# Weight folding around a branch: four pairs ahead of it instead of two, four buffers, and unread matrix products

## The chip, the cores and the metric

The kernel runs on one core of a Trainium2 chip. The metric is the device time of one execution in microseconds (us). Three runs of the kernel before took 677.29, 679.67 and 687.41 us; the median is 679.67 us. All times inside the kernel come from one profiled execution of the same kernel and are counted from the start of its span.

## The reference, cut to what matters

Two layers work on 800 tokens (8 batches of 100) of width 512, with a context of 361 rows of width 128:

```
x = x + L0_xattn(layernorm(x), ctx)      # 16 heads, causal mask over the first 100 context rows
x = x + L0_ffn(layernorm(x))             # 8 experts, each token to its best 2
x = x + L1_xattn(layernorm(x), ctx)      # low-rank queries, see below
x = x + L1_ffn(layernorm(x))             # weights and activations rounded to 8-bit steps
```

The part that matters here is the query path of the third line:

```
q_hk  = (hidden_q @ Wq.T).reshape(b, s, H, K)          # 16 heads of 128
q_big = einsum('bshk,hkq->bshq', q_hk, w_kc_q)         # to 384
q_r   = einsum('bshq,hqr->bhsr', q_big, W_qr)          # to 64 per head
```

None of the three matrices depends on the input, so the kernel multiplies them into one matrix `wqf` (512 x 1024) first, two heads ("a pair") at a time: eight pairs in all. This is called folding. Folding needs nothing but weights, so it can be put wherever TensorE would wait. The mixture of experts is the second line:

```
scores = einsum('btd,ed->bte', x, Wg)
topk_s, topk_i = top_k(scores, 2)
probs = softmax(topk_s)
y += w[..., e] * (silu(x @ W1[e].T) * (x @ W2[e].T)) @ W3[e].T     # for each expert e
```

## The kernel before, in words

TensorE (PE), VectorE (DVE) and ScalarE (ACT) run in the order in which the source writes their instructions (`tc.manual_schedule`); SyncE's queue (SP) issues nearly all transfers, and GpSimd (POOL) the indirect ones. A tile scheduler orders SP's transfers; in the built program each SP transfer waits for the one eight before it, as eight semaphores go round.

**Folding a pair.** `fold_load` (L698) issues five transfers for a pair on SP: `wq_p` (512 KB), and for each of two heads `kq_p` (192 KB) and `qr_p` (96 KB): 1088 KB. `fold_first` (L722) makes six products 128x64 (`kq_p` by `qr_p`, L711, twelve matmul instructions in the trace) and copies the result to `a_p` with ACT (L719). `fold_second` (L746) multiplies `a_p` by `wq_p` (L749, four instructions) and copies it to `f_p` with ACT (L753). `fold_third` (L756) turns `f_p` with four transposes (L759) and copies into `wqf` with ACT (L760). Inside the experts, `fold_beside` (L727, L731) and `fold_turn` (L739, L741) replace `fold_first`. The pool `fold_in` (L493) has three buffers for a pair's weights.

**Ahead of the branch.** After the first attention the kernel ranks the experts for each token. Tiles 0 to 4 of 128 tokens go first, tiles 5 and 6 later: `gate_norm` (L557) writes a normalised tile on DVE and issues a transfer `x_acc<-x` on SP; `gate_columns` (L569) transposes (L578), `gate_scores` (L586) makes the scores (L593, L601), `rank_choices` (L611) picks two experts with a chain of small DVE operations, `give_slots` (L653) counts with two products (L658, L661) where a token goes, and issues one indirect write on POOL per tile and choice (L686, 13 in all) into `x_slot` in HBM. Weights of experts 0 and 1 and of fold pairs 0, 1, 2 are loaded before that. Between the steps the kernel folds pair 0 and, later, pair 1. Pair 3 is loaded once pair 0 has been folded.

**The branch** (L906 to L1004). If an expert got more than 240 tokens, a loop handles what did not fit. With these inputs it is not entered; every engine reads one number (`spilt`, L831) and jumps past it.

**Behind the branch.** SP fetches the rows of experts 0 and 1 from `x_slot` (`fetch`, L1012; L1015), which needs the last indirect write to have landed; behind them three `gu` tiles and one `dn` tile of the last layer's weights, and pair 4 (`while len(loaded) < 3`, L1082). PE folds pairs 2 and 3 meanwhile, and then transposes the rows of expert 0 (`columns_of`, L1035; L1040).

**The experts** (L1102). For each: gate and up products in three parts (L1109), down products (L1175), scaling, and an indirect add into `x_acc` on POOL (L1186). Expert 0 to 3 each fold one pair between these steps (pairs 4 to 7, `fold_beside` behind the first of the three parts), and each issues the load of a later pair. DVE also rounds the last layer's weights there: two `gu` tiles per expert (`quantise_next`) and, in experts 0 to 3, one `dn` tile (`quantise_down`, L147 first) between the second and the third part's multiplication (L1133). There is one buffer for `dn`, so tile n+1 is loaded once tile n is rounded and turned. Weights of expert e+2 are loaded when expert e has finished with the buffer (`load_expert`, L482), and from expert 5 on the loads `wo` (L1070) use fold buffers that have come free.

Of the kernel before, what the change touches and what calls it, by code (L numbers as in the profile page):

```python
# [12 lines left out]
F32 = mybir.dt.float32  # L13
# [6 lines left out]
P = 128  # L20
# [30 lines left out]
def tile_kernel(  # L51
# [438 lines left out]

    fw, close_fw = open_pool("fold_in", bufs=3, side="right")  # L493
    wqf = fold.tile([P, KC, NH1 * R1], F32, tag="wqf", name="wqf")

    gp, close_gp = open_pool("gate", side="right")
# [225 lines left out]
    def fold_first(*loads):  # L722
        pa = fold_head(*loads, 0)
        return fold_copy(*loads, fold_head(*loads, 1, pa))
# [34 lines left out]
            nc.tensor.transpose(pt[:, ts(c, P)], f_p[:, ts(c, P)], ident)  # L759
        nc.scalar.copy(wqf[:, :, ts(i, P)], pt.rearrange("p (c r) -> p c r", c=KC))  # L760

    pairs_left = list(range(3, NH1 // 2))
    loaded = [fold_load(i) for i in range(3)]


    begin(6)
# [36 lines left out]
    project_part(5, po, oT, wout_sb, KC, 0, KC)  # L803
    rank_choices(0, 5)
    give_slots(0, 5)
    part = fold_first(*loaded.pop(0))
    project_add(5, po)
    token_stats(mvs, 5, 6)
    token_scales(mvs, sd_all, rstd_all, 5, 7)
    nc.scalar.activation(sd0[:, 0:1], ln_eps, AF.Exp)  # L810
    for t in range(5, 7):
        gate_norm(t)
    part = fold_second(*part)
    loaded.append(fold_load(pairs_left.pop(0)))
    xT = gate_columns(5, 7)
    fold_third(*part)
    gate_scores(5, 7, xT)

    part = fold_first(*loaded.pop(0))
    rank_choices(5, 7)  # L820
    give_slots(5, 7)

# [6 lines left out]
    nc.vector.tensor_reduce(most, pn[:, :NE], AX.X, ALU.max)  # L829
    spilt = gp.tile([P, 1], I32, tag="spilt", name="spilt")  # L830
    nc.vector.tensor_scalar(spilt, most, float(CAP), None, ALU.is_gt)  # L831
    part = fold_second(*part)
    fold_third(*part)
    close_atw()
    close_at()

# [76 lines left out]
    with tc.If(spills > 0, preferred_fallthrough_block=True):  # L913


        sp, close_sp = open_pool("spill", side="right")
        wts = sp.tile([P, NT, NE], F32, tag="wts", name="wts")
        for k in range(2):
            nc.vector.scalar_tensor_tensor(
                probs[k], slot1[k], 0.0, probs[k], ALU.is_equal, ALU.mult  # L920
            )
            nc.vector.tensor_tensor(
                hots[k], hots[k], probs[k].unsqueeze(2).to_broadcast([P, NT, NE]), ALU.mult
            )
        nc.vector.tensor_tensor(wts, hots[0], hots[1], ALU.add)
        full = N // P
        nc.gpsimd.memset(xs[0], 0.0)
        nc.gpsimd.dma_start(
            x_all_rows[: full * P].rearrange("(t p) d -> p t d", p=P), x_all[:, :full, :D]
        )  # L930
        nc.gpsimd.dma_start(x_all_rows[full * P : N], x_all[: N - full * P, full, :D])
        nc.gpsimd.dma_start(x_all_rows[N:], xs[0][: NR - N])
        for e in range(NE):
            nc.gpsimd.dma_start(
                spilt_gates[ds(e * NR, NR)].rearrange("(t p) o -> p t o", p=P),
                wts[:, :, e].unsqueeze(2),
            )

        at_w = sp.tile([P, KC + 3], I32, tag="at_w", name="at_w")
        nc.gpsimd.iota(at_w[:, :KC], pattern=[[P, KC]], base=0, channel_multiplier=1)  # L940
        nc.gpsimd.iota(at_w[:, KC:], pattern=[[P, 3]], base=0, channel_multiplier=1)
        at_x = sp.tile([P, 1], I32, tag="at_x", name="at_x")
        at_g = sp.tile([P, 1], I32, tag="at_g", name="at_g")
        nc.gpsimd.iota(at_g, pattern=[[0, 1]], base=0, channel_multiplier=1)

        def gathered(dst, src, at):
            nc.gpsimd.indirect_dma_start(
                out=dst, out_offset=None, in_=src,
                in_offset=bass.IndirectOffsetOnAxis(ap=at, axis=0),
            )  # L950

        with tc.For_i(0, NE, 1, hint_engines=()):
            nc.gpsimd.iota(at_x, pattern=[[0, 1]], base=0, channel_multiplier=1)
            w12_e = sp.tile([P, KC, 2 * HE], F32, tag="spw", name="spw")
            for c in range(KC):
                gathered(w12_e[:, c, :], w12.rearrange("e d h -> (e d) h"), at_w[:, c : c + 1])
            w3_e = sp.tile([P, 3, D], F32, tag="sp3", name="sp3")
            for m, (m0, mr) in enumerate(HCH):
                gathered(
                    w3_e[:mr, m, :], w3.rearrange("e h d -> (e h) d"),  # L960
                    at_w[:mr, KC + m : KC + m + 1],
                )
            nc.vector.tensor_scalar(at_w[:, :KC], at_w[:, :KC], D, None, ALU.add)
            nc.vector.tensor_scalar(at_w[:, KC:], at_w[:, KC:], HE, None, ALU.add)
            with tc.For_i(0, NT, 1, hint_engines=()):
                x_t = sp.tile([P, D], F32, tag="spx", name="spx")
                gathered(x_t, x_all_rows, at_x)
                g_t = sp.tile([P, 1], F32, tag="spg", name="spg")
                gathered(g_t, spilt_gates, at_g)
                pt = bank()  # L970
                for c in range(KC):
                    nc.tensor.transpose(pt[:, ts(c, P)], x_t[:, ts(c, P)], ident)
                xT = sp.tile([P, KC, P], F32, tag="spxT", name="spxT")
                nc.scalar.copy(xT, pt.rearrange("p (c q) -> p c q", c=KC))
                hT = sp.tile([P, 3, P], F32, tag="sph", name="sph")
                for m, (m0, mr) in enumerate(HCH):
                    pw = bank()
                    ups = [(0, UP[m], mr)] if m < 2 else [(0, UP64, 64), (64, HE, 32)]
                    for j, cols in enumerate(([(0, m0, mr)], ups)):
                        for to, at_col, n in cols:  # L980
                            for c in range(KC):
                                nc.tensor.matmul(
                                    pw[ds(to, n), ds(j * P, P)], w12_e[:, c, ds(at_col, n)],
                                    xT[:, c, :], start=(c == 0), stop=(c == KC - 1),
                                )
                    s = sp.tile([P, P], F32, tag="sps", name="sps")
                    nc.scalar.activation(s[:mr], pw[:mr, :P], AF.Silu)
                    nc.vector.tensor_tensor(hT[:mr, m, :], s[:mr], pw[:mr, ds(P, P)], ALU.mult)
                py = bank()
                for m, (m0, mr) in enumerate(HCH):  # L990
                    nc.tensor.matmul(
                        py[:, :D], hT[:mr, m, :], w3_e[:mr, m, :], start=(m == 0), stop=(m == 2)
                    )
                y_t = sp.tile([P, D], F32, tag="spy", name="spy")
# [84 lines left out]
    behind_slots.__enter__()  # L1079
    gate_up_in = [load_gate_up(gate_up_left.pop(0)) for _ in range(GB)]  # L1080
    down_in = load_down(0)
    while len(loaded) < 3:  # L1082
        loaded.append(fold_load(pairs_left.pop(0)))


# [4 lines left out]
    in_order.__enter__()  # L1090

    nc.scalar.activation(most, ln_eps, AF.Silu)
    part = fold_first(*loaded.pop(0))
    following = fold_first(*loaded.pop(0))
    part = fold_second(*part)
    following = fold_second(*following)
    fold_third(*part)
    fold_third(*following)
    turned = columns_of(0, slots[0])
    gates = choices(0, slots[0])  # L1100

# [709 lines left out]
```

## Time and profile before

| | us |
|---|---|
| median of three runs | 679.67 |
| profiled execution, device time | 681.28 |
| its span | 679.5 |
| PE busy | 646.9 (95%) |
| DVE busy | 419.9 (62%) |
| ACT busy | 245.0 (36%) |
| POOL busy | 183.5 (27%) |
| mean granted TensorE clock | 0.973 of full |

The profiled execution is 1.61 us above the median, and 1.78 us of it lie outside its span. Busy PE is not PE at its peak: at half clock the same products count twice the busy time. A line of the timeline reads: start, duration, engine, source line, operation, output and inputs, shape, how many instructions the line merges, and in brackets how long the engine was idle before it and what ended that. "SPq" is the issue of a transfer, not the transfer itself. In the table of stretches each row gives, after its length, the busy time and the number of instructions for PE, weight loads, DVE, ACT and POOL, and then the granted clock, the mean busy share of the 16 DMA engines, and GB/s.

### The profile page before, as it was taken

The numbers are of one execution on the slowest core, as the hardware profiler recorded it, in microseconds if no ns is written. First come the engines' busy times: TensorE is split into PE (matmuls) and PEld (weight loads), VectorE is DVE, ScalarE is ACT, GpSimd is POOL, SyncE is SP. The second block draws the span as 40 slices with busy tenths as digits, with TensorE's granted clock in tenths as the row PEclk, the third lists the DMA queues.
The fourth block names the chain that finished last, engine by engine and source line by source line (L and its number), as shares of the span: only waits on it lengthen the run. The fifth ranks groups of instructions, "written<-read, shape, count | busy, mean of one in ns | idle before, by whom it ended". The sixth has DMA issues, their size and how long they took to land.

```text
span 679.5 us, 9904 instructions
## 1 busy us (share of the span) xinstructions
PE 646.9 (95%) x3476; PEld 415.3 (61%) x3483; DVE 419.9 (62%) x1065; ACT 245.0 (36%) x565; POOL 183.5 (27%) x196
## 2 busy tenths in 40 slices
PE   8999997889998999999989999999999999999994
PEld 5766755666655677568866666666666544444442
DVE  4875697326655553353148877876677356666687
ACT  3654544322222111232145555555555313222140
POOL 2222231501110122138514243244234102221020
PEclk9999999589999999999989999999999999999998
DMA  9700393699999998654200211110000210011211
GB/s 292 249 18 17 119 322 108 241 309 220 299 295 302 253 326 214 140 175 120 84 1 15 59 44 21 53 36 12 0 13 0 90 38 20 18 30 29 49 37 63
DMA packets 80290, 80.35 MB, mean 118 GB/s; under 512 B 41267, under 2 KB 54119, under 8 KB 80111
## 3 DMA queue, kind: packets, MB, share of 16 engines
q1 hardware_dynamic: 76543, 70.97, 36.6%
q0 software_dynamic: 3696, 8.72, 6.0%
q8 instruction: 29, 0.48, 0.3%
q14 instruction: 22, 0.18, 0.1%
HBM read 56.36 MB, written 16.50 MB: 107 GB/s over the span
## 4 chain that ended last, share of the span: by engine, by line
PE 63%; DVE 7%; DMA 7%; POOL 1%; issue 1%; ACT 1%; SPq 0%; ACTq 0%; POOLq 0%; DVEq 0%
PE bank L359 12%; PE bank L1406 9%; PE bank L1379 9%; PE bank L1109 8%; PE bank L1325 6%; PE bank L1175 5%; PE bank L1394 5%; PE bank L1539 3%; DMA dn<-in_wdn 2%; PE bank L1361 1%; DMA gu<-in_wgu 1%; DMA qr_p<-in_wqr 1%; POOL e L1388 1%; DVE amax L147 1%; PE bank L711 1%
## 5 line engine op out<-in xcount | busy, mean ns | idle before, releaser
L1388 POOL TENSOR_SCALAR e<-e,rs 128x361 f32<-128x361 f32 (+1 forms) x56 | 67.2, 1201 | 131.9 <-DVE rs L1387 118.7
L359 PE MATMUL bank<-wvo,ctxT 128*128 128x512 f32 x192 | 83.9, 593 | 0.0
L1379 PE MATMUL bank<-kvT,qe 128*128 128x361 f32 (+1 forms) x208 | 83.0, 483 | 0.1
L1109 PE MATMUL bank<-xgT,w 128*128 128x240 f32 (+1 forms) x384 | 76.5, 373 | 1.6 <-ACT xgT L1044 0.9
L1109 PEld LDWEIGHTS bank<-xgT,w 128*128 128x128 f32 (+1 forms) x384 | 64.7, 183 | 14.4 <-issue 5.6
L1406 PE MATMUL bank<-pT,kvr 121*128 121x400 f32 x192 | 70.3, 502 | 1.0 <-DVE pT L80 1.0
L1394 PEld LDWEIGHTS bank<-ident,e 128*121 128x121 f32 (+1 forms) x312 | 48.3, 186 | 34.2 <-POOL e L1388 7.3
L1385 ACT ACTIVATE e<-bank,nm 128x361 f32<-128x361 f32 (+1 forms) x104 | 58.7, 565 | 27.2 <-DVE nm L1381 18.9
L1381 DVE TENSOR_REDUCE nm<-bank 128x1 f32<-128x361 f32 (+1 forms) x104 | 54.9, 528 | 15.8 <-PE bank L1379 14.6
L359 PEld LDWEIGHTS bank<-wvo,ctxT 128*128 128x128 f32 x192 | 36.2, 190 | 43.0 <-issue 42.6
L1186 POOL DMA_INDIRECT x_acc<-y,place x16 | 24.5, 1530 | 129.9 <-ACT y L1185 126.2
L1394 PE MATMUL bank<-ident,e 128*121 128x128 f32 (+1 forms) x312 | 53.0, 280 | 3.1 <-POOL e L1388 3.0
L1556 POOL TENSOR_TENSOR hid<-g,u 128x512 f32<-128x512 f32 (+1 forms) x17 | 20.5, 1216 | 111.0 <-ACT g L1547 74.8
L1175 PE MATMUL bank<-w,hT 128*128 128x512 f32 (+3 forms) x96 | 44.3, 607 | 4.0 <-DVE hT L1133 4.0
L1406 PEld LDWEIGHTS bank<-pT,kvr 121*128 121x128 f32 x192 | 33.9, 190 | 20.2 <-ACT pT L82 0.7
L1325 PE MATMUL bank<-xT,wqf 128*128 128x256 f32 (+1 forms) x192 | 43.8, 389 | 0.7 <-ACT xT L1310 0.7
L82 ACT COPY pT<-bank 121x384 f32<-121x384 f32 (+1 forms) x63 | 28.2, 447 | 42.4 <-PE bank L1394 42.3
L324 POOL TENSOR_TENSOR s<-s,rs 100x800 f32<-100x800 f32 x16 | 24.4, 1522 | 70.0 <-DVE rs L323 30.5
L1325 PEld LDWEIGHTS bank<-xT,wqf 128*128 128x128 f32 x192 | 36.3, 190 | 7.4 <-ACT xT L1310 0.9
L80 DVE COPY ctxT<-bank 128x400 f32<-128x400 f32 (+2 forms) x31 | 17.7, 572 | 37.0 <-PE bank L1325 26.0
L1379 PEld LDWEIGHTS bank<-kvT,qe 128*128 128x128 f32 (+1 forms) x208 | 32.9, 189 | 10.7 <-DVE rs L1387 0.5
L1175 PEld LDWEIGHTS bank<-w,hT 128*128 128x128 f32 (+3 forms) x96 | 16.8, 184 | 25.1 <-issue 16.6
(259 smaller groups left out, 1004.2 us busy)
## 6 DMA issues: line engine op xcount, KB each, us to landing
w<-in_w SPq DMA_DIRECT2D x8, 1408.0 KB
gu<-in_wgu SPq DMA_DIRECT2D x22, 256.0 KB
w<-in_w SPq DMA_DIRECT2D x16, 256.0 KB
wq_p<-in_wq SPq DMA_DIRECT2D x8, 512.0 KB
wo<-in_wo SPq DMA_DIRECT2D x8, 512.0 KB
x_slot<-zeros SPq DMA_DIRECT2D x1, 3840.0 KB
kq_p<-in_wkcq SPq DMA_DIRECT2D x16, 192.0 KB
dn<-in_wdn SPq DMA_DIRECT2D x4, 704.0 KB
```

The costliest lines, as they stand in the source:

```text
L82: nc.scalar.copy(dst, src)
L359: nc.tensor.matmul(po[:, :D], lhs[:, c, ds(t * P, r)], rhs[:, c, :], start=(c == 0), stop=(c == chunks - 1),)
L1109: nc.tensor.matmul(po, w12_e[:, c, cols], xgT[:, c, :], start=(c == c0), stop=(c == c1 - 1))
L1175: nc.tensor.matmul(py[i][:n], hT[:mr, m, ds(s0, n)], w3_e[:mr, m, :], start=(m == 0), stop=(m == 2))
L1186: d = nc.gpsimd.indirect_dma_start(out=x_acc, out_offset=bass.IndirectOffsetOnAxis(ap=place[:, 0:1], axis=0), in_=y, in_offset=None, compu ...
L1325: nc.tensor.matmul(pq[:, i, :], wqf[:, c, ts(p0 + i, P)], xT[:, c, :], start=(c == 0), stop=(c == KC - 1),)
L1379: nc.tensor.matmul(ps[:r, :L], qe[:, ds(k0, r)], kvT, start=True, stop=True)
L1381: d = nc.vector.tensor_reduce(nm[:r], ps[:r, :L], AX.X, ALU.max, negate=True)
L1385: nc.scalar.activation(e[:r], ps[:r, :L], AF.Exp, bias=nm[:r], accum_out=sm[:r])
L1388: (nc.vector if odd else nc.gpsimd).tensor_scalar_mul(e[:r], e[:r], rs[:r])
L1394: nc.tensor.transpose(pt[:LP, c, :r], e[:r, ds(c * (LP - 1), LP)], ident[:r, :r])
L1406: nc.tensor.matmul(pc[:, :VC], kvr[:, c, :], pT[:, c, :], start=(c == 0), stop=(c == LC - 1))
```

## The change

Four pairs are loaded at the start instead of three, into four buffers; pairs 0 to 3 are folded ahead of the branch and only pair 4 behind it; pairs 5, 6 and 7 are all loaded right behind the branch, and folded in experts 0, 1 and 2. Behind the branch four products 128x512 whose results nobody reads stand between the steps of pair 4 and before the rows' transposes. They multiply `ident` with a part of expert 0's weights, which are long loaded. To make room, the loop for tokens that do not fit uses older tiles as buffers; it is not entered here.

```
-    fw, close_fw = open_pool("fold_in", bufs=3, side="right")
+    fw, close_fw = open_pool("fold_in", bufs=4, side="right")
...
-    pairs_left = list(range(3, NH1 // 2))
-    loaded = [fold_load(i) for i in range(3)]
+    pairs_left = list(range(4, NH1 // 2))
+    loaded = [fold_load(i) for i in range(4)]
...
     give_slots(0, 5)
-    part = fold_first(*loaded.pop(0))
+    pair0 = fold_first(*loaded.pop(0))
     project_add(5, po)
...
     for t in range(5, 7):
         gate_norm(t)
-    part = fold_second(*part)
+    pair0 = fold_second(*pair0)
     loaded.append(fold_load(pairs_left.pop(0)))
+    pair1 = fold_first(*loaded.pop(0))
     xT = gate_columns(5, 7)
-    fold_third(*part)
+    pair1 = fold_second(*pair1)
     gate_scores(5, 7, xT)
 
-    part = fold_first(*loaded.pop(0))
+    pair2 = fold_first(*loaded.pop(0))
+    fold_third(*pair0)
+    fold_third(*pair1)
     rank_choices(5, 7)
     give_slots(5, 7)
...
-    part = fold_second(*part)
-    fold_third(*part)
+    pair2 = fold_second(*pair2)
+    pair3 = fold_first(*loaded.pop(0))
+    fold_third(*pair2)
+    pair3 = fold_second(*pair3)
+    fold_third(*pair3)
...
-    while len(loaded) < 3:
+    behind_branch = loaded.pop(0)
+    while pairs_left:
         loaded.append(fold_load(pairs_left.pop(0)))
...
-    part = fold_first(*loaded.pop(0))
-    following = fold_first(*loaded.pop(0))
-    part = fold_second(*part)
-    following = fold_second(*following)
-    fold_third(*part)
-    fold_third(*following)
+
+    def at_work(n):
+        for _ in range(n):
+            nc.tensor.matmul(bank(), ident, experts[0][0][:, 0, :512], start=True, stop=True)
+
+    pair4 = fold_first(*behind_branch)
+    at_work(1)
+    pair4 = fold_second(*pair4)
+    at_work(1)
+    fold_third(*pair4)
+    at_work(2)
+    part = None
     turned = columns_of(0, slots[0])
```

In the built program's order on SP, the five transfers of pair 3 now stand ahead of the writes `x_acc<-x` of tiles 2, 3, 4 and 6, and the fifteen transfers of pairs 5, 6 and 7 stand between the first `dn` tile and the fetch of expert 2's rows. The loads of expert 2's gate and up weights move behind the transpose of the first rounded `dn` tile, and each `wo` load moves up by one expert.

More of the change, by code (lines that the diff above doesn't have):

```diff
@@ L937, in tile_kernel @@
             )
+        w12_at = x_all.rearrange("p t w -> p (t w)")[:, : KC * 2 * HE]
+        w12_at = w12_at.rearrange("p (c h) -> p c h", c=KC)
         at_w = sp.tile([P, KC + 3], I32, tag="at_w", name="at_w")
@@ L953, in tile_kernel @@
             nc.gpsimd.iota(at_x, pattern=[[0, 1]], base=0, channel_multiplier=1)
-            w12_e = sp.tile([P, KC, 2 * HE], F32, tag="spw", name="spw")
+            w12_e = w12_at
             for c in range(KC):
                 gathered(w12_e[:, c, :], w12.rearrange("e d h -> (e d) h"), at_w[:, c : c + 1])
-            w3_e = sp.tile([P, 3, D], F32, tag="sp3", name="sp3")
+            w3_e = xs[1:4]
             for m, (m0, mr) in enumerate(HCH):
                 gathered(
-                    w3_e[:mr, m, :], w3.rearrange("e h d -> (e h) d"),
+                    w3_e[m][:mr], w3.rearrange("e h d -> (e h) d"),
                     at_w[:mr, KC + m : KC + m + 1],
@@ L965, in tile_kernel @@
             with tc.For_i(0, NT, 1, hint_engines=()):
-                x_t = sp.tile([P, D], F32, tag="spx", name="spx")
+                x_t = xs[4]
                 gathered(x_t, x_all_rows, at_x)
@@ L991, in tile_kernel @@
                     nc.tensor.matmul(
-                        py[:, :D], hT[:mr, m, :], w3_e[:mr, m, :], start=(m == 0), stop=(m == 2)
+                        py[:, :D], hT[:mr, m, :], w3_e[m][:mr], start=(m == 0), stop=(m == 2)
                     )
-                y_t = sp.tile([P, D], F32, tag="spy", name="spy")
+                y_t = xs[5]
                 nc.vector.tensor_scalar(y_t, py[:, :D], g_t, None, ALU.mult)
```

## The prediction

> **What bounds the kernel now.** PE is busy 95% of the span, so I looked first for where it is not, or is slow. The page's slices show one clock dip that matters, at 119 to 136 us, the place of the change.
>
> ```profile
> PEclk9999999589999999999989999999999999999998
> ```
>
> (One digit per 17 us.) Then the table of stretches: where the clock changed, and how much PE worked in some stretches of 3.41 us.
>
> ```profile
> 117.60:117.70 0.10, 0.00 (x0) 0.00 (x0) 0.10 (x1) 0.10 (x1) 0.00 (x0) 0.89 1.18 221
> 141.50:141.60 0.10, 0.10 (x2) 0.10 (x1) 0.00 (x0) 0.10 (x1) 0.00 (x0) 0.66 0.76 307
> ...
> 353.10:353.20 0.10, 0.10 (x4) 0.10 (x3) 0.00 (x0) 0.00 (x0) 0.00 (x0) 0.98 0.00 0
> 356.60:356.70 0.10, 0.10 (x3) 0.10 (x2) 0.10 (x1) 0.00 (x0) 0.00 (x0) 0.96 0.00 0
> ...
> 114.28:117.69 3.41, 1.29 (x6) 0.27 (x5) 2.77 (x12) 2.17 (x4) 2.21 (x2) 1.00 0.45 123
> 216.67:220.09 3.42, 0.99 (x3) 0.51 (x4) 3.20 (x9) 0.00 (x0) 0.00 (x0) 1.00 1.10 346
> 131.34:134.76 3.42, 3.42 (x18) 3.42 (x17) 0.00 (x0) 1.06 (x3) 0.26 (x1) 0.50 0.33 81
> 138.17:141.58 3.41, 3.41 (x14) 1.71 (x11) 0.00 (x0) 1.68 (x3) 0.00 (x0) 0.50 1.03 323
> ```
>
> The clock (third from the right) falls at 117.69, rises at about 141.53, falls at 353.20, rises at 356.60. These lie 23.84, 211.67 and 3.40 us apart, near multiples (7, 62, 1) of 3.41: the clock is set on a grid. It fell behind a cell with 1.29 us of PE (L711, L749), yet not behind one with 0.99 us of wide products (L1175); a cell full of L711, 64 columns each, did not lift it, a cell of L749 and transposes did. Wide products count, fold products little.
>
> The timeline then gives the events around the branch:
>
> ```profile
> 118.19 1.68 PE L578 MATMUL bank<-ident,x_all 128*128 128x128 f32 x8 [2.27 <-DVE x_all L560]
> 130.69 0.91 POOL L686 DMA_INDIRECT x_slot<-x_all,to  x1 [0.30 <-DVEq L913]
> 131.02 5.36 PE L711 MATMUL bank<-qr_p,kq_p 128*128 128x64 f32 x24 [1.01 <-PEq L913]
> 134.54 1.76 SPq L1015 DMA_DIRECT2D xg<-x_slot  x4
> 141.63 0.99 PE L1040 MATMUL bank<-ident,xg 128*128 128x128 f32 x8
> 148.62 0.87 PE L731 MATMUL bank<-kq_p,qr_p 128*64 128x128 f32 x10 [0.91 <-DMA qr_p<-in_wqr]
> ```
>
> POOL's thirteen indirect writes run nearly back to back from 115.05 to 131.6, and their landing frees the row fetch at 134.54. PE folds pairs 2 and 3 at half clock until 141.6, does not wait for rows, then waits at L731 for pair 4. The chain of waits shows that this is transfers, and so are two later stalls:
>
> ```profile
> 136.48 4.65 DMA gu<-in_wgu
> ...
> 141.14 7.44 DMA qr_p<-in_wqr
> ...
> 182.76 8.93 DMA dn<-in_wdn
> ...
> 207.03 6.35 DMA dn<-in_wdn
> ```
>
> After those `dn` landings PE waits 0.87 us (expert 2, at 197.42) and 2.88 us (expert 3, at 219.10) for L1133, which DVE does behind `quantise_down`. From 222 to 277 PE runs without a gap.
>
> **Part by part, on the profiled execution's own clock.**
>
> Loading pair 3 early: 1088 KB, 3.3 us at the 330 GB/s of 100 to 104 us. DMA carries only 87 and 18 GB/s at 104 to 112, and the `x_acc` writes it is put ahead of have no reader before the adds at 163. Cost 0. Pair 4 takes pair 3's old place, behind pair 0 (114.5).
>
> Folding ahead of the branch. Full-clock prices from pair 0: L711 1.52, L749 1.08; L759 at half clock 1.11, so about 0.6 (the expert stage has 0.60). Pair 1's L711 runs 115.9 to 117.4, in the 2.27 us gap; its cell then holds 2.8 us of PE instead of 1.29, so I take the clock to stay up. L749 of pair 1, which waits for its copy behind ACT's table load (to 118.7), pushes L593 by about 1 us; full-clock transposes (1.1 for 1.68) and sums win it back. Pair 2's L711 and two thirds (1.2) fit into the DVE chain of 2.7 us from score to L658. The last three indirect writes need their slots by 127.8; they waited 0.33 us, so rows come at most 0.3 earlier. Behind L658: 1.08 + 1.52 + 0.6 + 1.08 + 0.7 (ACT's copy) + 0.6, so PE reaches the branch at about 131.4 rather than 130.0, restarts 1 us later, at 132.4.
>
> Behind the branch: pair 4, 1.52 + 1.08 + 0.6, and four unread products. Their nearest row is L359, where eight instructions (four products) took 3.68 us: 0.92 each, 3.7 in all (6.7 at half clock, by L749's 1.98 to 1.08). That gives 139.0 to 139.3; before, it was 141.63. The rows are there: the transfers of pair 4 wait for the one eight before them, and `kq_p` issued at 138.76, so expert 0's two tiles had landed by about 138.7. So 2.6 us are won here, and the unread products cost at most 0.5.
>
> They are lost at once. Pair 5 now stands where pair 4 stood on SP: rows 968 KB, `gu` 768, `dn` 704, pair 1088, from 135.45 when bytes begin to flow. So L731 starts at 148.3 at best, while PE now arrives at about 144.4. Net gain here 0.3, with an idle 3.9 us instead of 1.2.
>
> That idle can drop the clock. A cell must keep about 1 us of wide work, so an idle of 3.9 escapes in 28% of phases: both ends must hold at least 1.48 of idle, 0.94 of 3.41. One cell at half clock costs up to 1.7 us, two 3.4, none 0: I take 1.6, towards one cell, as at 353.20.
>
> On the page "TensorE: Matmul & The Clock Gate" of the Trainium skill, section "Part 1: The HAM clock gate", the clock halves after a whole idle window of about 3.4 us and returns after one sustained busy window. By it, a gap of 2.27 us could not have halved the clock at 117.7 and 5.36 us of L711 should have restored it; the trace has both otherwise. By the rule an idle of 3.9 rarely holds a whole window, and the sum below would lose its 1.6.
>
> Experts 0 to 3. One pair less: expert 3 drops L731 0.81, L741 0.11, L749 0.86, L759 0.44 = 2.2 us of PE. Transfers: up to expert 2's `dn`, old and new order carry the same 12.9 MB (3.3 of folds plus an early 0.5 `wo` against 3.8 of folds), but pairs 6 and 7 now fill 152 to 158, where DMA moved 97, 260 and 185 GB/s: about 0.7 MB, 2.4 us. From there to expert 3's `dn`, 0.32 MB less (0.58 of pair 7 against 0.26 of `wo` parts), 1.1 us. So both landings come about 3.5 earlier. Bounds: PE gains 0.9 + 2.9 + 2.2 = 6.0 if `dn` keeps up, 0 if it doesn't move. Expert 2's weights are issued some 10 us later (165 for 155.68), and are read from 180: cover about 8 us, cost 0; with that cover gone, each us of delay is one of PE.
>
> Sum at expert 3's end: PE's own chain -0.3 + 1.6 - 6.0 = -4.7, but no earlier than `dn`, -3.5. Experts 4 to 7 and all behind are PE's own and move along. 681.28 - 3.5 = 677.8; the profiled run lies 1.6 above the median, so 676.2.
>
> **Rivals.**
>
> (a) Transfers set the end anyway. For: equal bytes up to expert 2's `dn`, and the `dn` transposes on SP take 4 to 8 us each behind whatever is queued. Against: the lull at 152. The gain shrinks to 0 to 1: about 679.
>
> (b) Everything comes true and neither the clock nor `dn` bites: -0.3 - 6.0 = -6.3, 673.4. Against: the 3.9 us idle.
>
> (c) Slower: the clock falls ahead of the branch all the same, since fold products did not lift it before. Then pair 1's L749 (1.98) and its third (1.11) stand ahead of L658, which comes 3.1 us late; slots, indirect writes and rows follow. Behind L658 come 2.82 + 1.98 + 1.1 + 0.7 more, behind the branch 10 to 13 us for 10.6. L731 comes 8 to 11 late. With all 6.0 regained later: +2; with none: +11. Middle +6, 685.7. It decides from the clock at 118 to 125. Against: the cell is fuller than 1.29, and all cells at 96 to 114 with transposes and narrow products held the clock.
>
> (d) The change doesn't do what it says: rows come later than the products' end, and the clock drops there. It costs 1 to 2, about 681.
>
> **How the numbers follow.** Forecast 0.42, (a) 0.18, (b) 0.12, (c) 0.20, (d) 0.08. I predict 676. The likeliest case alone spans 673 to 680. Range 668 to 687: below, (b) less the 1.6 us that a grid shift could save at 353 and the noise of the runs (2 to 8 us around their median); above, (c). Over 2% (13.6 us, about what these runs can tell from no change) needs (b) plus stretches the profile does not show, 0.08, or the upper end of (c) with a lasting half clock, 0.11. That leaves 0.81 within 2%.
>
> **What would show it.** Clock at full from 112 to 140 with L1040 near 139: the fold ahead of the branch is right; half clock at 118: (c). PE idle near 4 us before L731, ended by `qr_p`, at about 148: the give-back; none there would refute my queue reading. Half clock at about 148 to 152: the 1.6. In experts 2 and 3 no PE wait for L1133 over 1 us: the 3.5; waits as before: (a). Expert 2's first L1109 waiting for weights would break the cover I counted on.

## The result and the profile after

The changed kernel took 678.69 us (median of 20 runs, 675.34 to 686.19), the kernel before 677.31 us in the same runs (20 runs, 675.46 to 687.93). The ratio is 1.0019, with a 95% interval of 0.9996 to 1.0042: no change that can be measured. Measured once more (the third group below), it had 677.16 us against 677.65 for the kernel before, ratio 0.999 [0.9966, 1.0014]; square brackets give 95% intervals throughout. The forecast of 676.0, "same" at 0.81, holds. The route to it does not, as the profile shows. The profiled execution took 677.96 us, 676.1 of them the span. The page's slices of the granted clock:

```profile
PEclk9999999569999999999989999999999999999998
```

The dip is where it was, deeper, and not gone as forecast. The timeline around the branch (start, duration, engine, line, and in brackets the idle time before and what ended it):

```profile
119.85 1.97 PE L749 MATMUL bank<-wq_p,a_p 128*64 128x512 f32 x4 [0.21 <-ACT f_p L753]
123.66 2.82 PE L711 MATMUL bank<-qr_p,kq_p 128*128 128x64 f32 x12
129.74 0.27 ACT L719 COPY a_p<-bank 128x128 f32<-128x128 f32 x1 [6.87 <-PE bank L828]
130.86 0.23 ACT L631 ACTIVATE x_all<-x_all 128x2 f32<-128x2 f32 x1
133.25 0.98 POOL L686 DMA_INDIRECT x_slot<-x_all,to  x1 [5.15 <-DVE tmp L671]
...
138.96 1.77 SPq L1024 DMA_DIRECT2D xg<-x_slot  x4
...
149.49 0.98 PE L1049 MATMUL bank<-ident,xg 128*128 128x128 f32 x8
...
154.80 0.88 PE L731 MATMUL bank<-kq_p,qr_p 128*64 128x128 f32 x12
```

Pair 1's L749 takes 1.97 us, so the clock is at half, from 119.3 to 146.6 by the clock's own records. The last three indirect writes wait 5.15 us (0.33 before) and the row fetch is issued at 138.96 (134.54 before). The rows' transposes start at 149.49 (141.63 before) and do not wait for the rows: the folds and unread products ahead of them, run at half clock, end only then. L731 starts 7.5 us later than before (147.31) and waits for nothing. From there on the waits of the experts are gone. TensorE's waits from 150 to 225 us (what waited, for what: us in total, times, longest):

```profile
PE bank L1125 <- ACT xgT L1053: 0.9, 1, 0.9
PE bank L1125 <- issue: 0.4, 1, 0.4
```

The 3.8 us that TensorE waited at the down products, for L1133, are not there. Expert 4 starts at 220.11, against 221.76 before.

**One number sums up the front.** The front is the stretch up to expert 0's first gate product. In thirteen of the fourteen profiles of this study the time is the start of expert 4's first gate product plus 456.8 to 458.3 us. The exception is the first profile of the kernel before (459.5), in which the clock fell once more at 220.08. So what counts is how the events ahead of expert 4 add up. All are in us, read from the timelines. The columns give starts: of the last three indirect writes, of the row fetch on SP, of the transposes of expert 0's rows, of the first gate product of experts 0 and 4. "Two experts" are the intervals from expert 0's first gate product to expert 1's, and from expert 3's to expert 4's.

| profile | last 3 writes | fetch | rows' transposes | expert 0 | two experts (0, 3) | expert 4 | time |
|---|---|---|---|---|---|---|---|
| before | 128.15 | 134.54 | 141.63 | 143.53 | 19.36, 21.67 | 221.76 | 681.28 |
| changed | 133.25 | 138.96 | 149.49 | 151.39 | 17.68, 15.82 | 220.11 | 677.96 |
| a1 no products | 133.42 | 139.01 | 146.75 | 149.48 | 19.06, 15.82 | 219.58 | 677.79 |
| a2 products ahead | 133.61 | 140.50 | 144.17 | 146.07 | 25.83, 15.82 | 222.94 | 680.10 |
| a3 pair 5 ahead | 133.40 | 138.79 | 149.41 | 151.31 | 17.69, 15.82 | 220.03 | 678.30 |
| a4 both | 133.04 | 138.82 | 143.72 | 145.62 | 17.69, 15.82 | 214.35 | 672.47 |
| b1 exp ahead | 128.26 | 134.91 | 138.17 | 140.11 | 26.27, 18.71 | 220.31 | 677.74 |
| b2 a4 + exp ahead | 128.32 | 134.56 | 139.91 | 141.81 | 17.68, 15.82 | 210.53 | 667.83 |
| b3 loads alone | 128.45 | 135.06 | 140.87 | 142.77 | 17.68, 19.50 | 215.17 | 672.29 |
| c0 before again | 131.91 | 138.34 | 144.27 | 146.17 | 21.59, 17.60 | 220.58 | 677.46 |
| c1 changed again | 132.91 | 138.54 | 145.73 | 147.63 | 19.48, 15.83 | 218.15 | 675.13 |
| c2 b1 + pair 5 ahead | 131.80 | 137.24 | 150.09 | 151.99 | 17.68, 15.82 | 220.71 | 678.87 |
| d1 b2 again | 128.72 | 134.79 | 140.32 | 142.22 | 17.69, 15.83 | 210.95 | 667.73 |
| d2 b2, none behind | 128.34 | 134.60 | 138.38 | 141.10 | 19.79, 15.82 | 211.92 | 669.72 |

Experts 1 and 2 took 17.6 each in all of them, save expert 2 in the first profile of before (19.59).

### The profile page after: what moved, and what is told of

Same layout as the page of the kernel before. It is cut to its first block, busy times and chain, and to the rows that moved or that the text cites. A ratio compares the mean times of both kernels' runs of the same rounds, so it can differ in the third digit from the quotient of the medians.

```text
span 676.1 us, 9935 instructions
## 1 busy us (share of the span) xinstructions
PE 650.1 (96%) x3490; PEld 416.7 (62%) x3490; DVE 419.2 (62%) x1065; ACT 244.8 (36%) x564; POOL 183.5 (27%) x196
## 4 chain that ended last, share of the span: by engine, by line
PE 69%; DVE 4%; DMA 2%; POOL 1%; issue 1%; ACT 1%; SPq 1%; ACTq 0%; POOLq 0%; DVEq 0%
PE bank L359 12%; PE bank L1125 11%; PE bank L1422 10%; PE bank L1395 9%; PE bank L1341 6%; PE bank L1191 6%; PE bank L1410 5%; PE bank L1555 3%; PE bank L1377 2%; PE bank L1049 1%; POOL e L1404 1%; PE bank L1106 1%; DMA kv<-in_ctx_n 1%; PE bank L749 1%; DMA x_acc<-y,place 1%
## 5 line engine op out<-in xcount | busy, mean ns | idle before, releaser
L1125 PE MATMUL bank<-xgT,w 128*128 128x240 f32 (+1 forms) x384 | 75.1, 369 | 1.4 <-ACT xgT L1053 0.9
L80 DVE COPY ctxT<-bank 128x400 f32<-128x400 f32 (+2 forms) x31 | 17.7, 572 | 37.2 <-PE bank L1341 26.2
```

Source lines behind the costliest of these rows:

```text
L1125: nc.tensor.matmul(po, w12_e[:, c, cols], xgT[:, c, :], start=(c == c0), stop=(c == c1 - 1))
```

## The experiments

The runs came in four groups, the kernels of a group on one chip together with runs of the kernel before: its medians were 677.53, 674.94, 677.65 and 674.12 us. Every ratio is to the runs of its own group.

**First group: the unread products and pair 5's load.** Theory: the front's gain is lost at L731, which waits for pair 5, and in the clock behind that wait. Rivals: the unread products cost what they hide, or the front itself is late. The expectations call the first the clock theory and set a transfer theory beside it, by which the experts' transfers set the end whatever the front does.

a1, the changed kernel without its four unread products:

```
     pair4 = fold_first(*behind_branch)
-    at_work(1)
     pair4 = fold_second(*pair4)
-    at_work(1)
     fold_third(*pair4)
-    at_work(2)
```

> The changed kernel without the four unread products behind the branch. Clock theory (the fold ahead of the branch lets the clock fall, and the half clock eats what the expert stage wins): in the changed kernel's profile the products take 4.8 us of PE at half clock while the rows already lie there, but they also bring the clock back at 146.6. Without them expert 0's row transposes start 3 to 5 us earlier than 149.5, and the clock comes back later, in expert 0's first products, which then cost 2 to 3 us more; the start of expert 4 moves by -2 to +1 us. Transfer theory (the experts' transfers set the end, PE's front does not matter): expert 4 starts at 220.1 as before, ratio to the kernel before 1.00 to 1.005 either way.

678.82 us (676.45 to 679.55, 10 runs), ratio 1.0 [0.9966, 1.0034]. Without the products the rows' transposes start 2.74 us sooner, but expert 0 takes 1.38 more, at half clock until 152.28. Expert 4 gains 0.53. The products cost little here, and bring little.

a2, three more unread products ahead of the branch:

```
     pair0 = fold_second(*pair0)
+    at_work(1)
...
     xT = gate_columns(5, 7)
+    at_work(1)
...
     fold_third(*pair1)
+    at_work(1)
     rank_choices(5, 7)
```

> The changed kernel with three more unread products ahead of the branch: behind pair 0's second step, behind the row transposes, and ahead of the slot counts (about 2.8 us of PE at full clock). Clock theory: the clock stays at full from 112 to 140, the last three indirect writes follow the first ten within 1 us (5.15 us in the changed kernel), the row fetch is issued at 134 to 135.5 instead of 139.0, row transposes start near 139 to 140; PE then waits 2.5 to 4 us for pair 5 at L731, which starts near 148 to 149 instead of 154.8; expert 4 starts 4 to 6 us earlier than 220.1, and the ratio to the kernel before is 0.992 to 0.997. Transfer theory: rows come earlier, expert 4 starts within 1 us of 220.1. A third possibility, that the products do not hold the clock: it falls all the same, L658 comes 5 us later still, and the ratio is above 1.004.

681.08 us (675.66 to 687.06, 10 runs), ratio 1.0028 [0.9979, 1.0078]. Ahead of the branch the clock was at half from 126.51 to 129.92 only, and the rows' transposes came 5.3 us earlier than in the changed kernel. But the row fetch came at 140.50 instead of the 134 to 135.5 expected, and expert 4 starts 2.8 us later than in the changed kernel instead of 4 to 6 earlier. TensorE's timeline after the transposes:

```profile
146.07 3.48 PE L1129 MATMUL bank<-xgT,w 128*128 128x240 f32 x16 [0.92 <-ACT xgT L1061]
153.77 0.61 PE L731 MATMUL bank<-kq_p,qr_p 128*64 128x128 f32 x2 [4.21 <-DMA qr_p<-in_wqr]
154.87 1.51 PE L731 MATMUL bank<-kq_p,qr_p 128*64 128x128 f32 x10 [0.49 <-DMA qr_p<-in_wqr]
156.31 5.63 PE L1129 MATMUL bank<-xgT,w 128*128 128x240 f32 x16
```

This is the give-back of the forecast: 4.7 us of waiting for `qr_p`, and then sixteen gate and up products at 5.63 us that take 3.51 at full clock. Expert 0 takes 25.8 us instead of 17.7.

a3, pair 5's load moved ahead of the branch, right behind pair 1's `fold_second`:

```
     pair1 = fold_second(*pair1)
+    loaded.append(fold_load(pairs_left.pop(0)))
     gate_scores(5, 7, xT)
```

> The changed kernel with pair 5 loaded ahead of the branch, into pair 1's buffer as soon as that is folded, instead of behind the first dn tile. Clock theory: where the clock falls, PE did not wait for pair 5 anyway, so the profile moves by less than 1 us; in executions where the clock holds, the wait of 3 to 4 us at L731 is gone, so the fastest executions fall below the changed kernel's 675.3, to 671 to 674, while the median moves little. Transfer theory: 1088 KB less behind the branch brings every later transfer 3.3 us earlier, and expert 4 starts 2 to 3 us earlier in every execution.

677.72 us (674.24 to 678.99, 10 runs), ratio 0.9983 [0.9947, 1.0018]. Nothing is gained: with the clock at half from 129.26 to 146.33 TensorE reaches L731 at 154.72, without a wait, as it did in the changed kernel's profile with pair 5 loaded late.

a4, a2 and a3 together:

> The three products ahead of the branch and pair 5's early load together. Clock theory: full clock, row fetch at 134 to 135.5, row transposes near 139 to 140, no wait at L731 (starts near 144 to 145), expert 4 starts 8 to 10 us earlier than 220.1, ratio to the kernel before 0.985 to 0.992. Transfer theory: the dn tiles of experts 2 and 3 come no earlier, PE waits for L1133's product again, and expert 4 starts at most 4 us earlier than 220.1.

672.39 us (671.46 to 674.3, 4 runs), ratio 0.9898 [0.9814, 0.9981]. L731 starts at 149.03 without a wait, expert 0 takes 17.7 us, and expert 4 starts 5.8 us before the changed kernel's (8 to 10 were expected; the row fetch came at 138.82, not by 135.5). Each part alone brings nothing that can be measured, both together five us.

**Second group: why are the slots late?** In all profiles of changed kernels so far the last three indirect writes began at 133.0 to 133.6, at half and at full clock. In the changed kernel ScalarE runs the exp of the second ranking (L631) behind pair 2's copy (L719), and that copy came at 129.5 to 130.1, long after TensorE's L711. New theory A: the order on ScalarE makes the slots late.

b1 moves the exp ahead of the copy on ScalarE and leaves TensorE's order as it is (L719 and L760 are cut off from their products):

```
-    pair2 = fold_first(*loaded.pop(0))
-    fold_third(*pair0)
-    fold_third(*pair1)
+    load2 = loaded.pop(0)
+    pa2 = fold_head(*load2, 1, fold_head(*load2, 0))
+    put0 = fold_turned(*pair0)
+    put1 = fold_turned(*pair1)
     rank_choices(5, 7)
+    pair2 = fold_copy(*load2, pa2)
+    fold_put(*put0)
+    fold_put(*put1)
     give_slots(5, 7)
```

> The changed kernel with ScalarE's order alone altered: the exp of the second ranking (L631) stands ahead of the copy of pair 2's a_p (L719) and of the two copies into wqf (L760); TensorE's and VectorE's orders are as in the changed kernel. Theory A: the last three indirect writes were late (133.25, where the kernel before had 128.15) because that exp was queued behind the a_p copy, which TensorE's completion released at 129.7 only. Then the exp runs at about 126.6, as its input is ready at 126.56; L666 at about 128.3; the last three writes from about 130 and the fetch of rows issued at about 135.6 (138.96). The transposes of the rows stay at about 149.5, since TensorE's own chain of folds and unread products ends there; the time stays at 678, give or take 1.5. Rival 1: every completion of TensorE is reported late between 124 and 129.8, whoever waits for it: the exp at 126.6, but L666, which waits for the counts of L658, not before 129.8, the last three writes from about 131.3, the fetch at 137. Rival 2: ScalarE itself stands still until 129.7: the exp at 129.7, and nothing else moves.

676.81 us (674.54 to 681.34, 10 runs), ratio 1.0023 [0.9986, 1.006]. The exp ran at 124.86 and the copy right behind it, at 124.97; the last three writes began at 128.26. The clock stayed full to 148.45. Theory A's "transposes at 149.5" was wrong by 11 us. TensorE's timeline:

```profile
138.17 1.02 PE L1062 MATMUL bank<-ident,xg 128*128 128x128 f32 x8
140.11 3.48 PE L1138 MATMUL bank<-xgT,w 128*128 128x240 f32 x16 [0.92 <-DVE one L1047]
148.10 0.40 PE L731 MATMUL bank<-kq_p,qr_p 128*64 128x128 f32 x2 [4.51 <-DMA qr_p<-in_wqr]
149.20 1.51 PE L731 MATMUL bank<-kq_p,qr_p 128*64 128x128 f32 x10 [0.70 <-DMA qr_p<-in_wqr]
150.64 5.78 PE L1138 MATMUL bank<-xgT,w 128*128 128x240 f32 x16
```

A front 11.3 us earlier than the changed kernel's, and expert 4 starts at 220.31, as there: 8.6 us go in expert 0, at L731 and in the clock behind it, and 2.9 in expert 3, which waits 2.4 us at its down products again.

b2, the same order of ScalarE in a4:

> The same altered order of ScalarE in the version with three unread products and pair 5's load ahead of the branch (672.39 us, rows fetched at 138.82, their transposes at 143.72 on rows alone). Theory A: the rows come 3.4 us earlier, their transposes at about 140.5, the time 669. Rival 1: 1.5 to 2 us earlier, 670.5. Rival 2: 672.4.

668.37 us (666.94 to 670.29, 7 runs), ratio 0.9902 [0.9873, 0.9931]. The clock stays full to 663.6. Against the kernel before of its own chip that is no better than a4 (0.9898): ScalarE's order brings nothing that can be measured.

b3, the loads of the changed kernel with the folds where they were before (pairs 0 and 1 ahead of the branch, 2 and 3 behind it) and no unread products:

```
-    pair1 = fold_first(*loaded.pop(0))
     xT = gate_columns(5, 7)
-    pair1 = fold_second(*pair1)
+    fold_third(*pair0)
     gate_scores(5, 7, xT)
-    pair2 = fold_first(*loaded.pop(0))
-    fold_third(*pair0)
-    fold_third(*pair1)
+    pair1 = fold_first(*loaded.pop(0))
...
-    behind_branch = loaded.pop(0)
+    behind_branch = [loaded.pop(0) for _ in range(2)]
```

> Four buffers and the loads of the changed kernel, with the folds where the kernel before had them: pairs 0 and 1 ahead of the branch, 2 and 3 behind it, 4 to 7 in experts 0 to 3, no unread products. Theory A (the gain of the changed kernel is that of its earlier loads, and its loss that of the folds moved ahead of the branch): the last three indirect writes follow at once at about 128.3, the transposes of the rows start at about 141.6 as before, no wait for dn or for pair weights in the experts, each of the first four experts takes about 17.6 us (before 19.4, 17.6, 19.6, 21.7), expert 4 starts at about 214 (before 221.8), the time is 670 to 672. Rival 1 (the moved fold, not the loads, carries the gain): expert 3 still takes about 21 us and the time is 675 to 677. Rival 2 (the early loads themselves delay the slots): the last writes start at 131 or later, the transposes at 145 or later, the time is 675.

676.9 us (671.12 to 680.29, 10 runs), ratio 1.003 [0.9996, 1.0064]. The profiled execution is near theory A's (672.29 us, expert 0 in 17.68, expert 4 at 215.17), but expert 3 took 19.50 us instead of 17.6, with one wait left:

```profile
212.50 1.98 PE L1181 MATMUL bank<-w,hT 96*128 96x512 f32 x4 [0.78 <-DVE hT L1139]
```

But it was one of the three fastest of ten, and the median shows no gain. The fastest three had a mean clock of 0.980 to 0.981, the others 0.972 to 0.978 (before: a median of 0.9785); where they lost it stays open.

**Third group: both kernels once more.** b1 has two things that the changed kernel's profile lacked, another order and a copy that comes on time. So the changed kernel (c1) and the kernel before (c0) were profiled again unaltered, on one chip, with c2, which is b1 and pair 5's load ahead (the line of a3).

> The changed kernel as it is, profiled once more, on one chip with the two others of this call. Theory A (ScalarE's order makes the slots late): pair 2's a_p copy again not before 129.5, the last three indirect writes again from about 133.2, the fetch of rows at about 139, no wait at L731. Rival (the late copy belongs to the executions that were profiled so far, not to the order): the copy within 0.2 us of the end of TensorE's L711 of pair 2, the last three writes from about 128.3, the fetch at about 135, TensorE's transposes between 138 and 142, and then the 4 to 5 us wait of L731 for pair 5 that the version with the exp ahead showed (5.2 us); expert 4 starts at about 220 all the same, and the time is the same.

> The kernel before, profiled once more. Its first profile had expert 4 start at 221.8 and a time of 681.28, which is above its median of 677.3; by the 457 to 458 us that lie behind expert 4's start in every profile of the variants, its median execution starts expert 4 at about 219.5. Expected: where the time is near the median, a wait at the first down products of experts 2 and 3 that is 1 to 2 us shorter, or no fall of the clock at 220; the front as before, rows' transposes at about 141.6.

> The changed kernel with ScalarE's altered order (the exp of L631 ahead of pair 2's a_p copy) and pair 5's load ahead of the branch, without any unread product ahead of the branch. Theory A (the wait at L731 and the lost clock behind it are what gives the gain of the front back): the transposes of the rows at about 138.2 as with the altered order alone, no wait at L731, 17.6 us for each of experts 0 to 2 and 15.8 for expert 3, expert 4 at about 209, the time 667 give or take 2. Rival (the unread products ahead of the branch carried the gain of the two versions that had both): the clock falls to half between 118 and 130, the transposes come after 142, the time is 672 or more.

c0: 677.85 us (677.07 to 680.15, 8 runs), ratio 1.0008 [0.9982, 1.0035]. From its timeline:

```profile
122.80 2.82 PE L711 MATMUL bank<-qr_p,kq_p 128*128 128x64 f32 x12
...
129.38 0.27 ACT L719 COPY a_p<-bank 128x128 f32<-128x128 f32 x1 [7.36 <-remote]
...
131.91 0.98 POOL L686 DMA_INDIRECT x_slot<-x_all,to  x1 [4.03 <-DVE tmp L671]
...
150.84 0.40 PE L731 MATMUL bank<-kq_p,qr_p 128*64 128x128 f32 x2 [1.20 <-DMA qr_p<-in_wqr]
```

and from the first profile of the same kernel:

```profile
122.75 2.82 PE L711 MATMUL bank<-qr_p,kq_p 128*128 128x64 f32 x12
...
125.61 0.27 ACT L719 COPY a_p<-bank 128x128 f32<-128x128 f32 x1 [3.65 <-PE bank L711]
...
128.15 0.98 POOL L686 DMA_INDIRECT x_slot<-x_all,to  x1 [0.33 <-DVE tmp L671]
...
147.31 0.40 PE L731 MATMUL bank<-kq_p,qr_p 128*64 128x128 f32 x2 [0.29 <-DMA qr_p<-in_wqr]
```

The kernel before has the late copy too: in c0 L711 ends at 125.62 by its row, and the copy that it releases starts at 129.38 (125.61 in the first profile). The rows' transposes come 2.6 us later, L731 waits 1.8 us in all, expert 0 takes 21.6 us, and no expert waits for `dn`. So the lateness is not the change's, and theory A, which has it from the change's order on ScalarE, falls. Of the expectation, the missing waits and the missing fall at 220 came true; the front "as before" did not.

c1: 677.16 us (675.13 to 686.3, 10 runs), ratio 0.999 [0.9966, 1.0014]. From its timeline:

```profile
122.11 1.55 PE L711 MATMUL bank<-qr_p,kq_p 128*128 128x64 f32 x12
...
128.14 0.27 ACT L719 COPY a_p<-bank 128x128 f32<-128x128 f32 x1 [6.57 <-remote]
...
132.91 0.98 POOL L686 DMA_INDIRECT x_slot<-x_all,to  x1 [4.97 <-DVE tmp L671]
...
145.73 0.99 PE L1049 MATMUL bank<-ident,xg 128*128 128x128 f32 x8
...
151.76 0.40 PE L731 MATMUL bank<-kq_p,qr_p 128*64 128x128 f32 x2 [0.66 <-DMA qr_p<-in_wqr]
```

The same lateness at full clock (L711 in 1.55 us, over at 123.66). Late completions are in both c0 and c1, so this pair is the fairest comparison of profiles, though c1's profiled execution (675.13) is the fastest of its ten: the change's front is 1.5 us later, its expert 0 is 2.1 shorter, its expert 3 1.8 shorter, and expert 4 starts 2.4 earlier. The medians of the two (677.85 and 677.16) do not show that.

c2: 678.5 us (675.06 to 679.68, 12 runs), ratio 0.9999 [0.9976, 1.0021]. Its rival held: the clock was at half from 120.06 to 147.37. From its timeline:

```profile
126.78 0.21 ACT L631 ACTIVATE x_all<-x_all 128x2 f32<-128x2 f32 x1 [3.51 <-DVE m L624]
130.20 0.27 ACT L719 COPY a_p<-bank 128x128 f32<-128x128 f32 x1 [3.21 <-PE bank L842]
130.34 0.17 DVE L666 TENSOR_TENSOR nb<-bank,base 128x16 f32<-128x16 f32 x1 [2.38 <-PE bank L842]
131.80 0.98 POOL L686 DMA_INDIRECT x_slot<-x_all,to  x1 [3.27 <-DVE tmp L671]
```

The exp ahead of the copy runs in time, yet VectorE's L666, which reads the counts that TensorE's L658 made (ended at 128.61 by its row), is held to 130.34. This is rival 1 of b1's expectation: it is TensorE's completions that reach the others late, whoever waits. The clock is not one profile's chance either: the mean clock was 0.974 to 0.983 in all 12 runs of c2, and 0.992 to 0.998 in the 6 of d1 below, which differs from c2 by the three unread products ahead of the branch alone.

**Fourth group: does the faster version hold, and what are the products behind the branch worth?** d1 is b2 again; d2 is b2 without the four unread products behind the branch (the edit of a1).

> The fastest version so far once more (three unread products and pair 5's load ahead of the branch, the exp of L631 ahead of pair 2's a_p copy; ratio 0.9902 on one chip). If TensorE's completions come in time here, the last three indirect writes start at 128.3, expert 0's gate product at 141.8, expert 4's at 210.5, and the time is 457.5 later, 668. If they are held again as in the two latest profiles of the changed kernel and the kernel before, the last three writes start at 131 to 133, expert 0 at about 145.5, expert 4 at about 214, the time is 671.5. In both cases the ratio is 0.990, give or take 0.003, since the kernel before loses to the same holding; the rival, that the gain belonged to the one chip, has 1.000.

> The same version without the four unread products behind the branch. Theory A (they only cost: the rows come at most 3.3 us after their fetch is issued): where the last three writes start at 128.3, the rows' transposes start at about 138 instead of 139.9 and expert 4 1.5 to 2 us earlier than with them; where the writes are late, the products lie in the wait and the times are equal within 0.5. Rival (they hold the clock): TensorE waits some 1 to 5 us for the rows, the clock falls to half before expert 0 or in it, expert 0 takes 19.5 us or more instead of 17.7, and the time is 2 to 8 us more than with them.

d1: 669.5 us (667.73 to 670.67, 6 runs), ratio 0.9932 [0.9912, 0.9951]. d2: 670.05 us (666.63 to 671.08, 6 runs), ratio 0.9924 [0.9898, 0.995]. Both beat the kernel before, by 0.7 to 0.8% (the changed kernel was not run in this group); d1's gain lies at the edge of the 1% give or take 0.3 expected. TensorE in d1 and then in d2:

```profile
140.32 0.99 PE L1071 MATMUL bank<-ident,xg 128*128 128x128 f32 x8
142.22 3.48 PE L1143 MATMUL bank<-xgT,w 128*128 128x240 f32 x16 [0.92 <-ACT xgT L1075]
```

```profile
138.38 1.81 PE L1071 MATMUL bank<-ident,xg 128*128 128x128 f32 x8
141.10 5.58 PE L1140 MATMUL bank<-xgT,w 128*128 128x240 f32 x16 [0.92 <-ACT xgT L1075]
```

Without the products the transposes start 1.94 us earlier, but at half clock (1.81 for 0.99, and 5.58 for 3.48), from 135.13 to 145.37. Expert 4 starts 0.97 later. In the profiles the products cost as theory A had it and pay as the rival had it; the medians cannot part the two versions.

## Why the forecast was right, and where it was wrong

**The total.** "Same" came true. The forecast's main mechanism, a front that is gained and then lost in the wait at L731, is real, but it stands in full in the variants b1 and a2, for 1.4 us in c1, and not at all in the changed kernel's first profile. "They are lost at once": L731 was to start at 148.3 after an idle of 3.9 us; in b1 it started at 148.10 after 4.51. The wait is what held the gain: with pair 5 loaded ahead as well, a2's time fell from 681.08 to a4's 672.39 on one chip. In a2, b1 and c1 it starts 13.27, 13.19 and 13.22 us after the row fetch is issued. In the changed kernel's first profile that bound is 138.96 + 13.2 = 152.2, and TensorE came at 154.80, past it. This is why the wait, which the forecast named as its own test, is missing there: the front was late, and the reading of SP's queue is not refuted. Fronts from 140.1 to 151.4 (expert 0 in the changed kernel twice, a1, a2 and b1) all end with expert 4 between 218.2 and 222.9.

**The step that failed** is "so rows come at most 0.3 earlier", with its tacit base that the slots' chain runs as in the one profile of before. Rows were fetched 4.4 us later. TensorE's completions reached ScalarE and VectorE 2 to 6 us late (first profile: L711 over at 126.48, copy at 129.74; a1: 123.85 and 129.91). That happens in some executions of both kernels, so the forecast, made from one execution without it, had no term for it. The same late copy made TensorE itself wait for L749, 1.66 us in the first profile and 2.81 in c1, and this and the half clock, not the rows, delayed the transposes. Rival (d), priced at 681, had rows later than the products' end; they were later, but not that late. The first profile is nearest to rival (c): half clock from 119.3, L731 late by 7.5 us (8 to 11 forecast). But (c) let at most 6.0 be regained behind that, and 9.1 were by expert 4's start.

**The clock ahead of the branch**, "I take the clock to stay up", because the cell would hold 2.8 us of PE: right in c1, where it stayed up until 128.28, after 2.6 us without work, and in b1, where nothing was late, until 148.45; wrong in the first profile, where it fell at 119.32. A cell is one period, 3.41 us, of the grid on which the clock changes. The cells of each, by the table of stretches (after the length: PE's busy time and instructions; clock third from the right), of the changed kernel's first profile:

```profile
115.91:119.32 3.41, 2.54 (x21) 2.03 (x20) 2.48 (x6) 2.42 (x5) 2.73 (x3) 1.00 0.86 235
```

and of c1:

```profile
114.63:118.04 3.41, 2.56 (x16) 1.61 (x16) 2.81 (x11) 2.40 (x4) 2.26 (x3) 1.00 0.58 161
118.04:121.45 3.41, 2.48 (x20) 1.10 (x20) 0.94 (x3) 2.71 (x7) 2.80 (x3) 1.00 1.05 318
121.45:124.87 3.42, 2.91 (x24) 2.63 (x24) 2.28 (x16) 0.13 (x1) 2.50 (x4) 1.00 1.02 391
```

The first profile's cell and c1's first two cover the same instructions with nearly the same busy time, cut 1.3 us apart: the clock fell behind a cell that holds the last 0.3 us of pair 0's L749 and otherwise L711 and transposes, and held behind two that each have a whole L749 of 512 columns (1.08 us). The visible difference is where the grid lies, so rival (c), at 0.20, was no remote case. What a cell must hold stays open. The forecast's "wide products count, fold products little" is not borne out: c1's third cell held with 2.91 us of L601, L711 and L759 and no L749, while the cell of before at 114.28, with a whole L749 but 1.29 us busy, did not. One reading behind that rule was wrong: the forecast had the clock survive 216.67 to 220.09 on "0.99 us of wide products". The kernel before, finer:

```profile
219.50:220.00 0.50, 0.50 (x2) 0.18 (x1) 0.43 (x3) 0.00 (x0) 0.00 (x0) 1.00 1.04 385
220.50:221.00 0.50, 0.50 (x2) 0.00 (x0) 0.47 (x2) 0.46 (x1) 0.00 (x0) 0.50 1.02 389
```

It fell right behind that cell, for 3.41 us, so the cell is no case of a clock that holds.

**Prices.** At full clock L711 took 1.55 (1.52 forecast), L749 1.08, L759 0.61 to 0.66 (0.6), and b1's rows' transposes started at 138.17 (139.0 to 139.3). The four unread products took 5.2 us in the changed kernel, mostly at half clock, and 4.1 at full clock in b1 (3.7 forecast); the delay of 0.5 forecast for them was 1.9 in d1 against d2.

**The clock behind L731** was mis-sized: 1.6 us were put down, towards one cell. In b1 and a2 it lasted two cells (6.8 us), and cost 2.3 on sixteen gate products (5.78 for 3.51) and 0.7 on L731 (1.51 for the 0.84 of c1), 2.9 in all.

**Experts.** Expert 3 without its fold: 15.82 instead of 17.60, 1.8 of the 2.2 forecast, with 0.4 of idle left at expert 4's first product. The landings of `dn`: the waits are gone in the changed kernel, as forecast, but they are gone in c0 as well. They were there with early fronts: expert 0 at 143.5 (before), 140.1 (b1) and 142.8 (b3), not at 146.2 (c0). Pairs loaded sooner take part of them away: b3 waits 0.8 in all where the kernel before waited 0.9 in expert 2 and 2.9 in expert 3, and with pair 5 ahead too (b2, d1, d2, expert 0 from 141.1) none is left. Expert 2's weights, said to be covered, never made TensorE wait. The early load of pair 3, put at 0, cost nothing that any profile shows.

**The sum.** 677.8 was forecast for the profiled execution and 677.96 measured: luck, since the terms are far off. The forecast was -2.6 in front, +2.3 at L731, +1.6 in the clock and -6.0 in the experts, of which the transfers were to allow -3.5 in all. Measured to expert 4's start: +7.9 at the rows' transposes, then 9.5 regained by it (1.7 in expert 0, 2.0 in expert 2, 5.9 in expert 3); and 1.7 more behind it, where the kernel before had its fall at 220.

## What to carry to other kernels

Ahead of the work that waits for a transfer, find when that transfer can land at the earliest, counted from what starts it (here 13.2 us from the row fetch): time won in front of it is lost there until the transfer moves too, and moving the transfer alone brought nothing while the front was late (a3, c2); only both did (0.990). Profile the kernel before twice: two executions of one kernel differed here by 2.6 us at the rows' transposes and by all of the `dn` waits, which is more than the change was worth. Work that is only there to hold the clock has to be checked against the same version without it: the three products ahead of the branch carried the gain (c2 against d1), the four behind it cost about what they brought (d1 against d2).

## What the runs showed of the hardware

Late completions: in eight profiles (the changed kernel twice, a1 to a4, c0, c2) TensorE's completions between about 121 and 130 us reached the other engines 1 to 6 us after the end that TensorE's rows show, most of them let go together at 128 to 130; in the six others, none. The tenth indirect write was issued at 126 to 128 in both kinds, and one chip showed both kinds (c0 to c2 with, d1 and d2 without). In the four groups it goes with the time of the kernel before: medians of 677.5 and 677.7 us in the two whose profiles have it, 674.9 and 674.1 in the two others. The first profile of the kernel before does not fit, as it has none in runs with a median of 677.3. TensorE's ends are modelled in these rows, but where nothing is held they fit: in b1 pair 3's L711 ends at 128.18 and its copy starts at 128.27. Whether the products themselves or only their completions are held, and by what, stays open; no run was made for it.

The clock's grid: its records show stretches of half clock ahead of 360 us of 3.41, 6.83, 10.24, 17.07, 20.48, 23.89 and 27.31 us, that is 1, 2, 3, 5, 6, 7 and 8 times 3.41. Over the 18 runs of the changed kernel below 686 us, the time grows by 0.33 us for each us at half clock (correlation 0.77; 675.3 and 675.4 us at a mean clock of 0.991, 679 to 685 at 0.976 to 0.978, but 678.0 at 0.974). The Trainium skill, page "TensorE: Matmul & The Clock Gate", section "Part 1: The HAM clock gate", has the clock halve after an idle window of that length. The falls at 119.32 in the changed kernel's first profile and at 128.28 in c1 came with less: the longest idle in the cell ahead was 0.9 and 2.6 us. Only the waits of 4.51 us in b1 and 4.21 in a2 could hold such a window; in the cells ahead of those falls, 145.04 to 148.45 and 150.40 to 153.82, 3.06 and 3.37 us were idle.
